# A selective scan's two halves joined into one scan of 1024 columns, with its decays produced two units ahead and half of them kept in SBUF

## The chip, the core and the metric

The kernel runs on one core of a Trainium2 chip. The metric is device time in microseconds (us) of one execution, from the first to the last instruction and what lies around them; lower is better. Three runs of the kernel before gave 3161.89, 3162.53 and 3166.35 us, median 3162.53.

## The reference

The input x has 8 images of 96 channels and 64 x 64 pixels, read as 8 sequences of L = 4096 tokens. Layer 0 is a Mamba block with a residual:

```
u = group_norm(x) as tokens                      # (8, 4096, 96)
xm, z = split(u @ in_proj_w.T)                   # 192 channels each
xm = silu(causal_conv4(xm) + conv_b)
dt, Bm, Cm = split(xm @ x_proj_w.T)              # 6, 16 and 16 columns
delta = softplus(dt @ dt_proj_w.T + dt_proj_b)
h_t = exp(delta_t * A) * h_{t-1} + delta_t * Bm_t * xm_t     # 192 channels x 16 states
y_t = sum over the 16 states of h_t * Cm_t  +  xm_t * D
x = x + layer_norm((y * silu(z)) @ out_proj_w.T)
```

Layer 1 works on the tokens: linear attention without softmax (6 heads; keys times values are summed over a whole sequence), then a feed-forward of 96 to 384 to 96 with weights and activations rounded to 8 and 16 bit floats; both have a layer norm before and a residual.

The recurrence h is what matters here. For each image it has 192 x 16 = 3072 independent rows, each 4096 steps long.

## The kernel before

**Tiling.** Images are taken in pairs (NP = 4 pairs, p), and a sequence in NCH = 8 chunks of T = 512 tokens (c), so there are 32 chunks in a row. Each chunk does its scans in NU = 24 *units* u. `where(u)` (L653) splits u into j (three groups of 64 channels), g (four groups of four states) and b (which image of the pair). A unit works on 128 partitions, four states times 32 channels, and on two halves h (the two sets of 32 channels of the 64), each 512 columns long: 1024 columns in all.

**A unit's work.** In `unit` (L711) a unit u needs:
- its decays `da` = exp(delta * A): two ACT activations of 512 columns (`decay`, L675 to L683). They read `dl`, which DMA has spread over the partitions, and write one PSUM bank each; the tag `da` has two banks, so the decay of half h of unit u+1 is produced as soon as the scan of half h of unit u has read that bank.
- its products `dbu` = delta * x * B: one POOL multiplication of 1024 columns, both inputs in SBUF (`products_b`, L659). It is issued three units ahead (AHEAD = 3) into four buffers, so that of u+3 waits for the scans of u-1.
- its scans: two DVE `tensor_tensor_scan` of 512 columns (L741), one for each half, which read `da` from PSUM and `dbu` from SBUF and write `hs` in SBUF. The first value of a half is 0.0 in the first chunk of a pair and otherwise the last column of the same unit in the chunk before, read from the tile `state`, into which ACT copies the last columns of both halves (L719, L722).
- its products with C: `pr` = hs * cc on DVE (L763), where `cc` is C spread over the partitions by TensorE into PSUM (L671). For the six units in `POOLED` (4, 5, 12, 13, 20, 21) POOL multiplies instead, one unit later (`pooled`, L770), with C spread by DMA into SBUF.
- its sums over the states: TensorE adds the `pr` of a pair of units into the PSUM bank `y` (`sums`, L688 to L698), four matmuls a pair. The sums of units 4 and 5, and of 12 and 13, are issued at units 8 and 16; units 20 and 21 have no such place, so their `pr` is computed and never added. `gate` (L707) then multiplies y by silu(z).

**Order.** The order of the instructions is written out by hand and each engine runs its own in that order. Between the units' own work stand the steps of other stages, by the table `STEPS`: the projections of the chunk after next (P, with Silu and Softplus, which need another table of ACT), the output projection and norms of the chunk before (E), the feed-forward of a chunk nine earlier (F0, F1), the attention's weights (W) and the next pair's group statistics (G). In a unit these come in two parts: part 0 before the scans, part 1 after them. `now("norms")` and `now("others")` release small POOL jobs that were put off. At unit SILU = 10 the decays of unit 12 are put early into the two spare banks `mp` and `mE`, ahead of ACT's Silu.

**PSUM and SBUF.** All eight PSUM banks are in use: cc and da two each, mp, mE, mF and y one each. After the last chunk the rest of E, W and F runs as a tail, in which many lanes of F work at a time and reuse buffers: `x2` takes those of `pr` and `b` in turn.

Of the kernel before, what the change touches and what calls it, by code (L numbers as in the profile page):

```python
# [23 lines left out]
RANK = 6  # L24
POOLED = (4, 5, 12, 13, 20, 21)
POOLED_G = 2
SILU = 10
ROWS_B = (16, 18, 20, 22)
AHEAD = 3

# [35 lines left out]
def tile_mamba_linear_attention_ffn(  # L66
# [41 lines left out]
    def view(t, shape):  # L108
# [8 lines left out]
            t = t.rearrange("p (a b c) -> p a b c", a=shape[1], b=shape[2])  # L117
        return t

    def psum(tag="mp"):  # L120
        return ps_all.tile([128, T], F32, tag=tag, name=tag, bufs=2 if tag in ("cc", "da") else 1)


    ident = const.tile([128, 128], F32, name="ident")
    make_identity(nc, ident)
    mhalf = const.tile([128, 8], F32, name="mhalf")
    nc.vector.memset(mhalf, -0.5)

    def rsqrt(out_, var, eps):

# [98 lines left out]


    def passing(shape, name):
        t = p2.tile([128, 2, T], F32, tag="pr", name=name, bufs=4)
        return view(t, shape)

    gamma = const.tile([128, C], F32, name="gamma")
# [417 lines left out]
    def where(u):  # L653
        return u // (2 * NG), (u // 2) % NG, u % 2
# [17 lines left out]
            cc, lhsT=sel[64:128, g, b], rhs=s["cs"][64:128, :], start=True, stop=True  # L672
        )

    def decay(s, u, h, bank=None):  # L675
        if ("da", u, h) in s:
            return
        j, g, b = where(u)
        da = psum(bank) if bank else ps_all.tile([128, T], F32, tag="da", name="da", bufs=2)
        s["da", u, h] = da  # L680
        nc.scalar.activation(  # L681
            da, s["dl", j][:, 2 * b + h, :], AF.Exp, scale=aneg[:, 2 * j + h, g : g + 1]
        )  # L683


# [22 lines left out]
        zs = s["zs"][:, j, :]  # L708
        nc.vector.tensor_mul(zs, s["y"], zs)  # L709

    def unit(s, prev, nxt, first, u, steps):  # L711
        def at(v):
            return (s, v) if v < NU else (nxt, v - NU)


        if u - 1 in POOLED:
            pooled(s, u - 1)
        if u:
            nc.scalar.copy(state["new"][:, u - 1, :], s.pop(("hs", u - 1))[:, :, T - 1])  # L719
        else:  # L720
            if prev is not None:
                nc.scalar.copy(state["new"][:, NU - 1, :], prev.pop(("hs", NU - 1))[:, :, T - 1])  # L722
            state["last"] = state.get("new")
            state["new"] = p2.tile([128, NU, 2], F32, tag="state", name="state")
        to, v = at(u + 1)
        if to is not None:
            rows_c(to, v)
        if u - 3 in POOLED and u % 2 == 0:
            sums(s, u - 3)
        if u % 2 == 0 and (u or prev is not None) and (u - 1) not in POOLED:  # L730
            sums(s if u else prev, (u or NU) - 1)
        now("norms")
        steps(u, 0)
        to, v = at(u + AHEAD)
        if to is not None:
            products_b(to, v)
        hs = s["hs", u] = p2.tile([128, 2, T], F32, tag="hs", name="hs", bufs=3)
        dbu = s.pop(("dbu", u))
        to, v = at(u + 1)
        for h in range(2):  # L740
            nc.vector.tensor_tensor_scan(  # L741
                hs[:, h, :], s.pop(("da", u, h)), dbu[:, h, :],
                0.0 if first else state["last"][:, u, h : h + 1], ALU.mult, ALU.add,
            )
            if to is not None:
                decay(to, v, h)
        now("others")

        new = u % (2 * NG) == 1
        if new and u > 1:  # L750
            gate(s, u // (2 * NG) - 1)
        elif new and prev is not None:
            gate(prev, NJ - 1)
        if u == SILU and (nxt is not None):
            for h in range(2):
                decay(s, u + 2, h, ("mp", "mE")[h])
        steps(u, 1)
        if new:
            skip(s, u // (2 * NG))
        if u in POOLED:  # L760
            return
        pr = s["pr", u] = p2.tile([128, 2, T], F32, tag="pr", name="pr", bufs=4)
        nc.vector.tensor_mul(  # L763
            pr, hs, s.pop(("cc", u)).unsqueeze(1).to_broadcast([128, 2, T])
        )
# [172 lines left out]
    def chain_f(p, c, b, banks, lane=None):  # L938

        bank = banks[0]  # L940
        x1d, t1d = kept[p, c]
        after = lane is not None

        def place(tag, out_tag, bufs):

            return dict(tag=out_tag, bufs=bufs) if after else dict(tag=tag, bufs=1)

        blk = slice(b * NK, (b + 1) * NK)
        x2 = p2.tile(
            [128, NK, C], F32, name="x2", **place(f"x2{b}", ("pr", "b")[(lane or 0) % 2], 4)  # L950
        )
# [14 lines left out]
        yield  # L966
        x2f = x2.rearrange("p k c -> p (k c)")
        nc.vector.tensor_add(x2f, ps[:, 0 : NK * C], x2f)  # L968
        norm = norm_stats(x2, NK, f"f{b}")
        yield  # L970
        bank = banks[1]
        o2 = p2.tile([128, NK, C], F32, name="o2", **place("o2", "hs", 3))
        for k in range(NK):
            normalise(o2[:, k, :], x2[:, k, :], norm, k)
        yield
        ps = psum(bank)
        for k in range(NK):
            nc.tensor.transpose(ps[0:C, k * 128 : (k + 1) * 128], o2[:, k, :], ident)  # L978
        yield
        qT = p2.tile([C, T], F8, name="qT", **place("qT", "zs", 2))  # L980
        nc.scalar.activation(qT, ps[0:C, :], AF.Copy, saturate=False)
        yield
        h8 = []
        h16 = []
        casts = []

        def hidden(m):
            ps = psum(bank)
            nc.tensor.matmul(
                ps, lhsT=w1T[:, m * 128 : (m + 1) * 128], rhs=qT, start=True, stop=True  # L990
            )
            return ps

        def rounded(m, ps):
            to = dict(tag=("du", "dl")[lane % 2] if after else "h16")
            h16.append(p2.tile([128, T], F16, name="h16", **to))
            nc.scalar.copy(h16[m], ps)  # L997

        def relu(m):
            if not m:  # L1000
                h8.append(p2.tile([128, 3, T], F8, name="h8", **place("h8", "xm", 2)))
            if after:
                nc.vector.tensor_scalar(  # L1003
                    h16[m], h16[m], b1q[:, m : m + 1], 0.0, ALU.add, ALU.max
                )
# [12 lines left out]
        ps = hidden(1)  # L1018
        yield
        rounded(1, ps)  # L1020
        relu(0)
        ps = hidden(2)
        yield
        rounded(2, ps)
        relu(1)
        yield
        relu(2)
        yield
        for job in casts:
            settle(job)  # L1030
        ps = psum(bank)
        for m in range(3):
            nc.tensor.matmul(  # L1033
                ps[0:C, :], lhsT=w2T[:, m, :], rhs=h8[0][:, m, :], start=(m == 0), stop=(m == 2)
            )
        yield
        y16 = p2.tile([C, T], F16, name="y16", **place("y16", "pq", 2))
        nc.scalar.copy(y16, ps[0:C, :])
        if after:
            nc.vector.tensor_scalar(y16, y16, b2q, None, ALU.add)  # L1040
        else:
            nc.scalar.activation(y16, y16, AF.Identity, bias=b2q)
        ps = psum(bank)
        for k in range(NK):
            nc.tensor.transpose(ps[0:C, k * 128 : (k + 1) * 128], x2[:, k, :], ident)  # L1045
        yield
        res = p2.tile([C, T], F32, tag="rows", name="res")
        nc.vector.tensor_add(res, ps[0:C, :], y16)  # L1048
        nc.sync.dma_start(out[2 * p + b, :, c * T : (c + 1) * T], res)
# [62 lines left out]
    with tc.manual_schedule():  # L1112
        for u in range(AHEAD):
            products_b(slots[0], u)
        for h in range(2):
            decay(slots[0], 0, h)
        rows_c(slots[0], 0)
        for i, (p, c) in enumerate(chunks):
            s = slots[i]
# [14 lines left out]
                    step(name, i)  # L1134

            for u in range(NU):
                unit(s, prev, nxt, c == 0, u, steps)

    for kind in list(waiting):
        now(kind)  # L1140
        del waiting[kind]
    s = slots[N - 1]
    sums(s, NU - 1)
    gate(s, NJ - 1)
    rest = [(p, c, b) for p in range(NP) for c in range(NCH) for b in range(2)]
# [81 lines left out]
```

## Time and profile before

| | us | share of the span |
|---|---|---|
| median of three runs | 3162.53 | |
| profiled execution, first to last instruction (span) | 3160.5 | |
| DVE busy | 2935.2 | 93% |
| POOL busy | 2840.7 | 90% |
| PE busy | 2469.6 | 78% |
| ACT busy | 2263.9 | 72% |
| PE weight loads | 928.7 | 29% |
| DMA, mean of 16 engines | | 57% in the main queue |

The engines are PE (TensorE), DVE (VectorE), ACT (ScalarE) and POOL (GpSimd); SP issues most DMAs. An engine's busy time is the union of its instructions, so that two which overlap by their ends are not counted twice. A group's row gives the line of the kernel, the engine, the operation, the tile written and those read, the shape, the count, then the busy time and the mean of one, and at last how long the engine sat idle just before instructions of this group, and what ended that idle time. The first scans start 69.5 us after the first instruction, and the last one ends at 3008.1 us; what follows is the tail. The granted TensorE clock is 0.81 of full speed on average.

### The profile page before, as it was taken

How to read it: one execution, taken by the hardware profiler on the slowest of the kernel's cores; microseconds unless marked ns; L12 is line 12 of the kernel's file. 1: busy time of each engine (PE TensorE's matmuls, PEld its weight loads, DVE VectorE, ACT ScalarE, POOL GpSimd, SP SyncE). 2: the span in 40 equal slices, each digit the busy share in tenths (PEclk: the TensorE clock that was granted, in tenths of full speed). 3: DMA queues.
4: the chain of work that ended last, by engine and by line, in shares of the span. 5: the costliest groups of instructions: out<-in, count | busy, mean ns of one | idle time of the engine just before them, and what ended most of it. 6: DMA issues, size and time to landing. Idle time of an engine off the chain costs nothing. (4 is left out here: it accounts for less than half of the span.)

```text
span 3160.5 us, 35127 instructions
## 1 busy us (share of the span) xinstructions
PE 2469.6 (78%) x9450; PEld 928.7 (29%) x9450; DVE 2935.2 (93%) x4265; ACT 2263.9 (72%) x4360; POOL 2840.7 (90%) x1921
## 2 busy tenths in 40 slices
PE   6787787878787777777777778777888778887777
PEld 2122222222222223222233323222323222332344
DVE  4999999999999999999999999999999999999945
ACT  3666666667677777777777777777877777777656
POOL 2999999999999999999999999999999999999955
PEclk8677777787778888888888877898888888877668
DMA  6655556665555667555667555567565466755322
GB/s 149 152 122 137 134 156 152 160 150 135 141 143 135 138 162 175 146 129 125 141 164 170 141 146 125 137 157 170 146 148 127 124 144 162 169 132 134 95 70 73
DMA packets 253037, 443.75 MB, mean 140 GB/s; under 512 B 37605, under 2 KB 45990, under 8 KB 252838
## 3 DMA queue, kind: packets, MB, share of 16 engines
q1 hardware_dynamic: 247846, 439.40, 56.9%
q10 hardware_dynamic: 4992, 2.11, 0.3%
q8 instruction: 74, 1.21, 0.2%
q14 instruction: 125, 1.02, 0.1%
HBM read 349.11 MB, written 92.27 MB: 140 GB/s over the span
## 5 line engine op out<-in xcount | busy, mean ns | idle before, releaser
L659 POOL TENSOR_TENSOR dbu<-du,b 128x1024 f32<-128x1024 f32 x768 | 1804.6, 2371 | 112.6 <-DVE hs L741 65.5
L741 DVE TENSOR_TENSOR_SCAN hs<-da,state,dbu 128x512 f32<-128x512 f32 x1290 | 1573.5, 1265 | 25.6 <-ACT da L681 24.6
L681 ACT ACTIVATE da<-dl,aneg 128x512 f32<-128x512 f32 x1474 | 1000.6, 688 | 665.4 <-DVE hs L741 644.2
L763 DVE TENSOR_TENSOR pr<-hs,cc 128x1024 f32<-128x1024 f32 x576 | 698.7, 1213 | 35.1 <-DVE hs L741 0.5
L695 PE MATMUL y<-pr,ssum 128*32 128x512 f32 x2816 | 585.1, 831 | 113.3 <-DVE pr L763 113.3
L770 POOL TENSOR_TENSOR pr<-hs,c 128x1024 f32<-128x1024 f32 x192 | 453.8, 2363 | 36.6 <-DVE hs L741 30.4
L459 PE MATMUL mp<-u,wk 96*64 96x512 f32 x1488 | 398.1, 658 | 66.6 <-ACT xm L477 66.4
L671 PE MATMUL cc<-cs,sel 64*128 64x512 f32 x576 | 330.0, 583 | 144.8 <-DVE pr L763 144.4
L671 PEld LDWEIGHTS cc<-cs,sel 64*128 64x128 f32 x576 | 121.6, 215 | 557.3 <-DVE pr L763 296.8
L741 DVE TENSOR_TENSOR_SCAN hs<-da,dbu 128x512 f32<-128x512 f32 x184 | 213.2, 1205 | 17.4 <-POOL dbu L659 9.9
L516 PE MATMUL mp<-dbl,dtT 12*128 12x512 f32 x186 | 158.9, 947 | 56.8 <-ACT cs L506 38.5
L695 PEld LDWEIGHTS y<-pr,ssum 128*32 128x32 f32 x2816 | 87.9, 132 | 380.6 <-DVE pr L763 201.6
L791 PE MATMUL mE<-woT,zs 128*128 128x192 f32 x744 | 146.6, 350 | 66.7 <-ACT t1e L799 45.1
L459 PEld LDWEIGHTS mp<-u,wk 96*64 96x64 f32 x1488 | 97.0, 145 | 293.6 <-issue 156.6
L132 POOL TENSOR_TENSOR rs<-rs,mhalf 128x8 f32<-128x8 f32 (+1 forms) x128 | 173.3, 1354 | 10.7
L791 PEld LDWEIGHTS mE<-woT,zs 128*128 128x128 f32 x744 | 127.3, 200 | 126.8 <-ACT t1e L799 70.5
L703 PE MATMUL y<-xm,dd 128*128 128x512 f32 x192 | 129.2, 760 | 22.4 <-DVE zs L709 21.9
L467 PE MATMUL mp<-u,wz 96*64 96x512 f32 x372 | 137.0, 825 | 4.3 <-ACT xm L485 4.3
L1011 POOL CAST h<-h 128x512 fp8e5<-128x512 f16 x192 | 117.6, 622 | 24.8 <-DVE h L1003 15.8
L719 ACT COPY state<-hs 128x2 f32<-128x2 f32 x736 | 130.1, 181 | 0.2
L420 ACT ACTIVATE o<-x,nm,rs 128x96 f32<-128x96 f32 x256 | 98.6, 455 | 36.4 <-POOL nm L414 34.4
L531 POOL TENSOR_TENSOR du<-delta,xm 128x512 f32<-128x512 f32 x93 | 117.1, 1273 | 0.0
(306 smaller groups left out, 3234.1 us busy)
## 6 DMA issues: line engine op xcount, KB each, us to landing
du<-lu SPq DMA_DIRECT2D x380, 256.0 KB, 5.5
dl<-ld SPq DMA_DIRECT2D x380, 256.0 KB, 7.9
b<-bd SPq DMA_DIRECT2D x512, 128.0 KB, 5.0
lu<-du SPq DMA_DIRECT2D x96, 256.0 KB, 5.7
ld<-delta SPq DMA_DIRECT2D x93, 256.0 KB, 2.4
c<-bd SPq DMA_DIRECT2D x128, 128.0 KB, 4.4
xg<-in_x_dram SPq DMA_DIRECT2D x32, 384.0 KB, 3.8
xr<-in_x_dram SPq DMA_DIRECT2D x32, 384.0 KB, 8.7
```

The source lines that it names most:

```text
L132: nc.gpsimd.tensor_tensor(out_, out_, mhalf[0 : out_.shape[0], 0 : out_.shape[1]], op=ALU.pow)
L459: nc.tensor.matmul(ps[64 * b : 64 * b + 64, :], lhsT=wk[:, k, 64 * j : 64 * j + 64], rhs=u[:, b, k : k + T], start=(k == 0), stop=(k == 3),)
L467: nc.tensor.matmul(ps[64 * b : 64 * b + 64, :], lhsT=wz[:, 64 * j : 64 * j + 64], rhs=u[:, b, 3 : T + 3], start=True, stop=True,)
L516: nc.tensor.matmul(ps, lhsT=dtT[:, j, :], rhs=dbl[0 : 2 * RANK, :], start=True, stop=True)
L659: nc.gpsimd.tensor_mul(dbu, s["du", j][:, 2 * b : 2 * b + 2, :], s["b", g][:, b, :].unsqueeze(1).to_broadcast([128, 2, T]),)
L671: nc.tensor.matmul(cc, lhsT=sel[64:128, g, b], rhs=s["cs"][64:128, :], start=True, stop=True)
L681: nc.scalar.activation(da, s["dl", j][:, 2 * b + h, :], AF.Exp, scale=aneg[:, 2 * j + h, g : g + 1])
L695: nc.tensor.matmul(s["y"][q : q + 32, :], lhsT=ssum, rhs=pr[:, h, :], start=False, stop=(g == NG - 1),)
L741: nc.vector.tensor_tensor_scan(hs[:, h, :], s.pop(("da", u, h)), dbu[:, h, :], 0.0 if first else state["last"][:, u, h : h + 1], ALU.mult, ...
L763: nc.vector.tensor_mul(pr, hs, s.pop(("cc", u)).unsqueeze(1).to_broadcast([128, 2, T]))
L770: nc.gpsimd.tensor_mul(pr, s["hs", u], s["c", g][:, b, :].unsqueeze(1).to_broadcast([128, 2, T]))
L791: nc.tensor.matmul(ps[:, 2 * k * C : 2 * (k + 1) * C], lhsT=zs[:, j, tok : tok + 128], rhs=woT[:, j].rearrange("p b c -> p (b c)"), start= ...
```

## The change

The two scans of a unit become one of 1024 columns over both halves, h = 0 first. To keep the halves apart, the decay of column 0 of the second half is a constant 0.0, written once. The second half's carried state then can't be the scan's first value; instead its share, exp(delta * A) of that column times the carried state, is added into the same column of `dbu` by a one-column ACT activation (`carry`), a unit ahead. The factors for that come from `first_decays`, four small ACT activations for each j of a chunk. In the first chunk of a pair there is nothing to carry.

The decays lie in two fixed tiles, used by turns: even units in PSUM (two banks, as before), odd units in a new SBUF tile `ds`. Those of unit u+2 are issued right after the scan of unit u. The rule for unit SILU goes. To find room in SBUF, the tag `pr` has three buffers in place of four, here, in the constants' set-up and in the tail. The missing sums of units 20 and 21 are added at unit 0 of the next chunk, and after the last chunk, so y now holds these two units' products.

```diff
-SILU = 10
+    das = [
+        ps_all.tile([128, 2, T], F32, tag="da", name="da"),
+        const.tile([128, 2, T], F32, name="ds"),
+    ]
+    for t in das:
+        nc.vector.memset(t[:, 1, 0:1], 0.0)
-        t = p2.tile([128, 2, T], F32, tag="pr", name=name, bufs=4)
+        t = p2.tile([128, 2, T], F32, tag="pr", name=name, bufs=3)
+    def decay(s, u):
         j, g, b = where(u)
+        for h in range(2):
+            nc.scalar.activation(
+                das[u % 2][:, h, h:T], s["dl", j][:, 2 * b + h, h:T], AF.Exp,
+                scale=aneg[:, 2 * j + h, g : g + 1],
+            )
+    def first_decays(s, j):
+        a0 = s["a0", j] = p2.tile([128, NG, 2], F32, tag="a0", name="a0")
+        dl = s["dl", j].rearrange("p (b h) t -> p b h t", h=2)
+        for g in range(NG):
+            nc.scalar.activation(
+                a0[:, g, :], dl[:, :, 1, 0], AF.Exp, scale=aneg[:, 2 * j + 1, g : g + 1]
+            )
+    def carry(s, u, last):
+        j, g, b = where(u)
+        if not u % (2 * NG):
+            first_decays(s, j)
+        to = s["dbu", u][:, 1, 0:1]
         nc.scalar.activation(
+            to, s["a0", j][:, g, b : b + 1], AF.Identity, bias=to, scale=last[:, u, 1:2]
         )
...
+        if u == 0 and prev is not None:
+            sums(prev, NU - 3)
...
-        to, v = at(u + 1)
-        for h in range(2):
-            nc.vector.tensor_tensor_scan(
-                hs[:, h, :], s.pop(("da", u, h)), dbu[:, h, :],
-                0.0 if first else state["last"][:, u, h : h + 1], ALU.mult, ALU.add,
-            )
-            if to is not None:
-                decay(to, v, h)
+        if u + 1 < NU:
+            if not first:
+                carry(s, u + 1, state["last"])
+        elif nxt is not None and not last:
+            carry(nxt, 0, state["new"])
+        nc.vector.tensor_tensor_scan(
+            hs.rearrange("p h t -> p (h t)"),
+            das[u % 2].rearrange("p h t -> p (h t)"),
+            dbu.rearrange("p h t -> p (h t)"),
+            0.0 if first else state["last"][:, u, 0:1], ALU.mult, ALU.add,
+        )
+        to, v = at(u + 2)
+        if to is not None:
+            decay(to, v)
         now("others")
...
-        if u == SILU and (nxt is not None):
-            for h in range(2):
-                decay(s, u + 2, h, ("mp", "mE")[h])
...
         x2 = p2.tile(
-            [128, NK, C], F32, name="x2", **place(f"x2{b}", ("pr", "b")[(lane or 0) % 2], 4)
+            [128, NK, C], F32, name="x2",
+            **place(f"x2{b}", ("pr", "b")[(lane or 0) % 2], 3 + (lane or 0) % 2)
         )
...
+    sums(s, NU - 3)
     sums(s, NU - 1)
```

More of the change, by code (lines that the diff above doesn't have):

```diff
@@ L118, in view @@
         return t
+    das = [
+        ps_all.tile([128, 2, T], F32, tag="da", name="da"),
+        const.tile([128, 2, T], F32, name="ds"),
+    ]
+    turns = [0]
     def psum(tag="mp"):
-        return ps_all.tile([128, T], F32, tag=tag, name=tag, bufs=2 if tag in ("cc", "da") else 1)
+        if tag == "da":
+            turns[0] += 1
+            return das[0][:, turns[0] % 2, :]
+        return ps_all.tile([128, T], F32, tag=tag, name=tag, bufs=2 if tag == "cc" else 1)
     ident = const.tile([128, 128], F32, name="ident")
@@ L673, in rows_c @@
         )
-    def decay(s, u, h, bank=None):
-        if ("da", u, h) in s:
-            return
+    def decay(s, u):
         j, g, b = where(u)
-        da = psum(bank) if bank else ps_all.tile([128, T], F32, tag="da", name="da", bufs=2)
-        s["da", u, h] = da
+        for h in range(2):
[15 more added lines that the diff above has]
+        to = s["dbu", u][:, 1, 0:1]
         nc.scalar.activation(
-            da, s["dl", j][:, 2 * b + h, :], AF.Exp, scale=aneg[:, 2 * j + h, g : g + 1]
+            to, s["a0", j][:, g, b : b + 1], AF.Identity, bias=to, scale=last[:, u, 1:2]
         )
@@ L709, in gate, with unit @@
         nc.vector.tensor_mul(zs, s["y"], zs)
-    def unit(s, prev, nxt, first, u, steps):
+    def unit(s, prev, nxt, first, last, u, steps):
         def at(v):
@@ L761, in unit @@
             return
-        pr = s["pr", u] = p2.tile([128, 2, T], F32, tag="pr", name="pr", bufs=4)
+        pr = s["pr", u] = p2.tile([128, 2, T], F32, tag="pr", name="pr", bufs=3)
         nc.vector.tensor_mul(
@@ L1114, in tile_mamba_linear_attention_ffn @@
             products_b(slots[0], u)
-        for h in range(2):
-            decay(slots[0], 0, h)
+        for u in range(2):
+            decay(slots[0], u)
         rows_c(slots[0], 0)
@@ L1136, in tile_mamba_linear_attention_ffn @@
             for u in range(NU):
-                unit(s, prev, nxt, c == 0, u, steps)
+                unit(s, prev, nxt, c == 0, c == NCH - 1, u, steps)
     for kind in list(waiting):
```

## The prediction

> **What bounds the kernel now.** I read the page's engine shares and its costliest groups first, then the table of busy time by stage, the waits of DVE, and at last the shortest and longest instruction of single lines. The page's groups (line, engine, operation, output from inputs, count; then busy us and mean ns of one; then idle time before them):
>
> ```profile
> L659 POOL TENSOR_TENSOR dbu<-du,b 128x1024 f32<-128x1024 f32 x768 | 1804.6, 2371 | 112.6 <-DVE hs L741 65.5
> L741 DVE TENSOR_TENSOR_SCAN hs<-da,state,dbu 128x512 f32<-128x512 f32 x1290 | 1573.5, 1265 | 25.6 <-ACT da L681 24.6
> L681 ACT ACTIVATE da<-dl,aneg 128x512 f32<-128x512 f32 x1474 | 1000.6, 688 | 665.4 <-DVE hs L741 644.2
> L763 DVE TENSOR_TENSOR pr<-hs,cc 128x1024 f32<-128x1024 f32 x576 | 698.7, 1213 | 35.1 <-DVE hs L741 0.5
> ```
>
> The scans and the products pr fill DVE, which hardly idles; ACT waits 644 us for scans, so it has room. The stages (us, then busy us and count of PE, PEld, DVE, ACT, POOL, then granted clock, DMA share, GB/s): start, body in four stretches, tail.
>
> ```profile
> 0.00:69.50 69.50, 41.85 (x136) 15.92 (x136) 25.70 (x79) 20.63 (x42) 13.21 (x37) 0.93 0.55 136
> 69.50:591.10 521.60, 412.46 (x1411) 131.68 (x1411) 509.66 (x608) 349.13 (x651) 482.50 (x256) 0.75 0.60 144
> 591.10:1512.10 921.00, 720.53 (x2782) 262.33 (x2782) 889.56 (x1226) 671.43 (x1283) 858.51 (x538) 0.82 0.60 146
> 1512.10:2638.00 1125.90, 894.99 (x3540) 335.75 (x3540) 1078.03 (x1546) 862.21 (x1658) 1057.48 (x702) 0.83 0.60 146
> 2638.00:3008.10 370.10, 285.57 (x1067) 109.47 (x1068) 355.30 (x500) 269.49 (x531) 345.14 (x231) 0.76 0.55 133
> 3008.10:3160.50 152.40, 114.16 (x515) 73.58 (x513) 76.93 (x312) 90.99 (x200) 83.85 (x160) 0.75 0.23 70
> ```
>
> In the body (2938.6 us) DVE is busy 2832.6 and POOL 2743.6. DVE sets the pace, and POOL idles only 195.0 us of it. Whatever makes POOL longer by more than that sets a new pace.
>
> **The change, part by part.** The sum is made against the profiled span, 3160.5 us; the median of the runs, 3162.53, lies 2.0 above it.
>
> *One scan in place of two.* Two scans of 512 in a row take 2.45 us by the timeline where they read a carried state and 2.33 where the first value is a constant; one alone takes 1.265 and 1.205, so the second adds 1.19 and 1.13. One scan of 1024 reads no state for its second half: that saves 0.06. It also saves the fixed part of a second instruction. DVE's products take 0.668 at 512 columns (zs, L709) and 1.213 at 1024, so at most 2 x 0.668 - 1.213 = 0.12 is fixed. The saving lies in 0.06 to 0.18 per unit with state (672 of 768) and 0 to 0.12 without (96): 40 to 132 us of DVE. I take the middle, 0.12 and 0.06: 86 us, and 2.33 for the long scan.
>
> *Decays two units ahead.* decay(u+2) still waits for scan u, whose buffer it overwrites, but the scan of u+1 no longer needs it. That aims at the idle time that DVE owes to ACT:
>
> ```profile
> DVE hs L741 <- ACT da L681: 31.7, 43, 1.2
> DVE res L1048 <- ACT da L681: 19.8, 18, 1.7
> ```
>
> So 0 to 51 us more. The rule SILU that goes had prefetched one unit into spare banks (62 decays), which now run in their ordinary turn.
>
> *ACT's additions.* 672 carries of one column and 28 x 3 x 4 = 336 first decays of two columns; the nearest row is the state copy (L719, 128x2), 181 ns: 1008 x 0.181 = 182 us. Half the decays now write SBUF; the nearest such row is the relu of L1007, 720 ns against 688, some 25 us. ACT goes from 2264 to about 2470 us, under POOL and DVE: nothing on the path by itself. The carry of u+1 waits for the product dbu of u+1, and behind it in ACT's queue stand decay(u+2), the state copy and the steps' evictions. When I set each product's end beside the scans in the timeline, the product of u+1 has ended before scan u starts in over nine cases of ten (median 2.9 us before), so today's lead of POOL covers it; if POOL becomes the pace this cover is gone, and ACT runs at POOL's heel.
>
> *The left-out pair.* The sums for units 20 and 21: L695 has 2816 records, 88 per chunk, 8 for a pair. 256 more at 585.1/2816 = 0.21 us are 53 us of PE, spread over chunks whose PE is busy 75 to 80%, and ahead of a gate that waits 4.7 us for PE in the whole run. Cost nothing to 5 us.
>
> *Three pr buffers for four, three x2 buffers in every second lane of the tail.* pr of u+3 needs the sums of u, issued a unit earlier: 0 to 10 us; in the tail a load waits for an older lane: 0 to 5. I take 5 in all, lost in the rest.
>
> *Half the decays in SBUF.* This decides. A scan of an odd unit now has both operands, ds and dbu, in SBUF, while POOL multiplies two SBUF tensors nearly without pause. Every large DVE row of the body today has one input in PSUM (da, cc, y, mE, mF) or only one input, so no row shows such a pair beside a product. From one side: nothing. From the other: the engines exclude each other, as the smallest row of the body shows for a DVE copy within SBUF. (Minimum, median and maximum ns of one, then the POOL instruction beside the slowest copy, and that copy; then POOL beside the last copy, and that copy):
>
> ```profile
> L170 DVE COPY gnm<-gnmv x4: 165/302/2003, 25.4 to 2094.6; 96x2 f32<-96x2 f32 x4
> ```
> ```profile
> 606.12 2.36 POOL L659 TENSOR_TENSOR dbu<-du,b 128x1024 f32<-128x1024 f32 x1 [1.96 <-DMA dl<-ld]
> ```
> ```profile
> 606.50 2.00 DVE L170 COPY gnm<-gnmv 96x2 f32<-96x2 f32 x1
> ```
> ```profile
> 2092.54 4.69 POOL L659 TENSOR_TENSOR dbu<-du,b 128x1024 f32<-128x1024 f32 x2
> ```
> ```profile
> 2094.62 0.30 DVE L170 COPY gnm<-gnmv 96x2 f32<-96x2 f32 x1
> ```
>
> A copy of two columns takes 165 ns at the start, with POOL idle. At 606.50 it meets a product that ends at 606.12 + 2.36 = 608.48, and ends 0.02 us later. At 2094.62 it meets the first of two products in a row; it ends as that one does (half of 4.69) and slips in between. So a product holds something that this copy needs, for its whole length, and DVE gets it at the product's end. The subtraction L176, two SBUF inputs, took 157 ns each time, but it only ever met POOL's power (L132), beside which the tail's relu (L1003) also ran at 353 ns, while beside casts that relu took up to 765. So L176 tells nothing. The row nearest to the new scan is the copy beside a product, so I take exclusion: an odd scan waits for the running product, and POOL stands still for the scan.
>
> The Trainium skill ("SBUF — State Buffer", "Who interferes with whom") says it directly: a DVE instruction with two SBUF inputs and a GpSimd instruction that reads SBUF exclude each other for the whole instruction. By it, the sum is the one below; no run here shows it yet.
>
> **The sum.** POOL stands still 384 x 2.33 = 895 us. Its power rows are 173.3 of 2840.7 us busy, 6%, beside which a scan would cost nothing: -54. Of POOL's 195 us idle, 143 is waiting for DVE's scans and statistics (65.5 + 30.4 + 47.1) and mostly goes when POOL is last; I leave 100 for that and for waits behind the carries. Start 69.5, body 2743.6 + 895 - 54 + 100, tail 152.4, around it 2.0: **3908 us**. DVE would need 2832.6 - 86 + 384 waits of 0 to 2.37 = 2747 to 3657 in the body, under POOL's 3685, so POOL sets the pace and DVE's saving is worth nothing. All idle gone: 3808. All idle kept and nothing free beside the power: 4057.
>
> **The rivals.**
> *No exclusion for two inputs* (the other side: faster). For it: scan and product read at a leisurely pace, over 2 ns a column each, and the copy's case may be its own. Against: the copy's rows. Then 3162.5 - 86 - 51 = 3026 at best; POOL's floor is 69.5 + 2743.6 + 152.4 + 2 = 2968, and with 100 of idle 3068, so DVE and POOL both stand near the limit: 3085, between 3026 and 3130. It decides if an odd scan costs POOL under (195 - 100)/384 = 0.25 us; above that POOL's body outgrows today's.
> *Shared reads without a lock.* A product makes 2048 reads a lane in 2.36 us, 1.15 ns each; if each of the scan's 1024 reads pushes one back, a scan costs POOL 1.18 us, 453 in all: 69.5 + 2743.6 + 453 + 100 + 152.4 + 2 = 3521, between 3300 and 3800.
> *The carry as the new wait.* Without exclusion, scans whose product comes late (about one in 15) wait through ACT: 50 units by up to 1.5 us, 75 us, and the gain shrinks to 3160: no change.
>
> **How the numbers follow.** Exclusion 0.74 (3800 to 4060 its own range, 0.66 within it, the rest above or just under); shared reads 0.10; no exclusion 0.13; carry 0.03, of which 0.02 within 0.2%, about what a measurement of this kernel can tell from no change, and 0.01 slower. Range 3300 to 4060: it holds the first and the second case but for their ends and leaves out the faster one. Faster 0.13, same 0.02, slower 0.85.
>
> **What would show it.** Right: scans from ds far longer than scans from da (toward 3.5 to 4.7 us, or an idle time before them), products of POOL with a mean over 3 us or gaps that end with a scan, POOL over 95% of the body, DVE's share down. Wrong: scans from ds and da alike near 2.33 and products still at 2.37. If the time is near 3500, products are stretched by about 1.2 us only beside scans from ds. I am wrong altogether if ACT is the last to end before scans.

## The result, and the profile after

The kernel after takes 3776.24 us (median of 4 runs, 3772.44 to 3776.61), beside 3162.21 us for the kernel before on the same chip: 1.193 times as long, interval 1.192 to 1.195. Slower, as forecast, inside the range but 132 us short of the 3908 foretold. The profiled execution has a span of 3770.6 us. In the kernel after, the lines have moved: the products `dbu` stand at L669, the scan at L773, POOL's `pr` at L802, the carry at L708.

First the groups of the page, to be held against those of before (busy us, mean ns of one, then idle time before them):

```profile
L669 POOL TENSOR_TENSOR dbu<-du,b 128x1024 f32<-128x1024 f32 x768 | 2174.2, 2852 | 47.3 <-DMA ld<-delta 36.0
L773 DVE TENSOR_TENSOR_SCAN hs<-ds,state,dbu 128x1024 f32<-128x1024 f32 x336 | 1099.6, 3273 | 97.3 <-ACT dbu L708 77.8
L773 DVE TENSOR_TENSOR_SCAN hs<-da,state,dbu 128x1024 f32<-128x1024 f32 x336 | 786.6, 2341 | 109.0 <-ACT dbu L708 77.7
...
L802 POOL TENSOR_TENSOR pr<-hs,c 128x1024 f32<-128x1024 f32 x192 | 607.3, 3163 | 2.5 <-issue 1.2
...
L708 ACT ACTIVATE dbu<-a,dbu,state 128x1 f32<-128x1 f32 x672 | 256.8, 382 | 168.5 <-POOL dbu L669 167.8
```

The same scan instruction takes 2.34 us where its decays lie in PSUM and 3.27 where they lie in SBUF. POOL's products, which have not changed, went from a mean of 2.37 to 2.85 us. The idle time of the products that scans had caused (65.5 us before) is down to 10.5. The stages (us, then busy us of PE, PEld, DVE, ACT, POOL, granted clock, DMA share, GB/s), start, body, tail:

```profile
0.00:70.10 70.10, 41.33 (x136) 15.93 (x136) 25.88 (x81) 21.66 (x44) 13.20 (x37) 0.93 0.52 134
70.10:3622.50 3552.40, 2613.21 (x9053) 919.71 (x9053) 3150.17 (x3108) 2405.85 (x5122) 3496.16 (x1723) 0.72 0.48 119
3622.50:3770.60 148.10, 109.72 (x519) 68.79 (x517) 78.38 (x311) 92.53 (x203) 84.06 (x161) 0.77 0.24 73
```

The whole loss lies in the body, 3552.4 us against 2938.6. POOL is busy in 3496.2 of it, so it idles 56 us: POOL has taken DVE's place as the engine that ends last. The instructions of single lines (minimum, median and maximum ns of one, then the times of the first and last) show that the loss is in the instructions and not between them:

```profile
L773 DVE TENSOR_TENSOR_SCAN hs<-ds,state,dbu x336: 2317/3118/4575, 172.9 to 3620.2; 128x1024 f32<-128x1024 f32 x168
L773 DVE TENSOR_TENSOR_SCAN hs<-da,state,dbu x336: 2317/2343/2352, 169.3 to 3616.6; 128x1024 f32<-128x1024 f32 x168
L669 POOL TENSOR_TENSOR dbu<-du,b x768: 2334/2362/4464, 67.7 to 3607.2; 128x1024 f32<-128x1024 f32 x192
L422 POOL TENSOR_SCALAR nm<-mv x128: 239/258/2596, 202.8 to 3749.0; 128x8 f32<-128x8 f32 x64, 128x4 f32<-128x4 f32 x64
L142 POOL TENSOR_TENSOR rs<-rs,mhalf x128: 1036/1398/1675, 203.5 to 3749.6; 128x8 f32<-128x8 f32 x64, 128x4 f32<-128x4 f32 x64
```

A scan from `da`, with one input in SBUF, takes 2.35 us at most, one from `ds` up to 4.58. A product's shortest and median time are those of an undisturbed one, its longest 2 us more. Even a multiplication of four columns by -1 (L422) can take 2.6 us. Only the power (L142) is untouched in this kernel. What happens is seen in a few us of the timeline (start and length in us), first POOL, then DVE:

```profile
1802.82 2.35 POOL L669 TENSOR_TENSOR dbu<-du,b 128x1024 f32<-128x1024 f32 x1
1805.13 4.35 POOL L802 TENSOR_TENSOR pr<-hs,c 128x1024 f32<-128x1024 f32 x1
1802.90 4.42 DVE L773 TENSOR_TENSOR_SCAN hs<-ds,state,dbu 128x1024 f32<-128x1024 f32 x1 [0.77 <-POOL pr L802]
1807.42 1.22 DVE L795 TENSOR_TENSOR pr<-hs,cc 128x1024 f32<-128x1024 f32 x1
```

The scan starts at 1802.90, while a product runs that ends at 1802.82 + 2.35 = 1805.17. It ends at 1807.32, 2.15 us after that product: an almost whole scan follows the product's end. POOL's next product starts at 1805.13 and ends at 1809.48, 2.16 us after the scan's end: it has waited inside its own instruction in turn. Over the whole run, 293 of the 384 scans that read `ds` ended 2.15 us after a running product's end (90% of these between 2.146 and 2.151), and 268 products that started during such a scan ended 2.14 to 2.18 us after it. These 268 took 4.24 to 4.46 us; the other 692 of the 960 products took 2.33 to 2.39, with none between.

### The profile page after: what moved, and what is told of

Read it like the earlier page. It is cut to its first block, busy times and chain, and to the rows that moved or that the text cites. A ratio compares the mean times of both kernels' runs of the same rounds, so it can differ in the third digit from the quotient of the medians.

```text
span 3770.6 us, 35419 instructions
## 1 busy us (share of the span) xinstructions
PE 2764.3 (73%) x9706; PEld 1004.4 (27%) x9706; DVE 3254.4 (86%) x3499; ACT 2520.0 (67%) x5368; POOL 3593.4 (95%) x1921
## 3 DMA queue, kind: packets, MB, share of 16 engines
q1 hardware_dynamic: 247846, 439.40, 47.1%
## 5 line engine op out<-in xcount | busy, mean ns | idle before, releaser
L669 POOL TENSOR_TENSOR dbu<-du,b 128x1024 f32<-128x1024 f32 x768 | 2174.2, 2852 | 47.3 <-DMA ld<-delta 36.0
L773 DVE TENSOR_TENSOR_SCAN hs<-ds,state,dbu 128x1024 f32<-128x1024 f32 x336 | 1099.6, 3273 | 97.3 <-ACT dbu L708 77.8
L773 DVE TENSOR_TENSOR_SCAN hs<-da,state,dbu 128x1024 f32<-128x1024 f32 x336 | 786.6, 2341 | 109.0 <-ACT dbu L708 77.7
L688 ACT ACTIVATE ds<-dl,aneg 128x512 f32<-128x512 f32 (+1 forms) x768 | 510.9, 712 | 406.2 <-DVE hs L773 396.1
L722 PE MATMUL y<-pr,ssum 128*32 128x512 f32 x3072 | 673.8, 894 | 136.1 <-DVE pr L795 131.6
L688 ACT ACTIVATE da<-dl,aneg 128x512 f32<-128x512 f32 (+1 forms) x768 | 527.6, 687 | 257.0 <-DVE hs L773 207.6
L802 POOL TENSOR_TENSOR pr<-hs,c 128x1024 f32<-128x1024 f32 x192 | 607.3, 3163 | 2.5 <-issue 1.2
L469 PE MATMUL mp<-u,wk 96*64 96x512 f32 x1488 | 519.9, 824 | 58.8 <-ACT xm L487 50.0
L708 ACT ACTIVATE dbu<-a,dbu,state 128x1 f32<-128x1 f32 x672 | 256.8, 382 | 168.5 <-POOL dbu L669 167.8
L142 POOL TENSOR_TENSOR rs<-rs,mhalf 128x8 f32<-128x8 f32 (+1 forms) x128 | 173.2, 1353 | 10.7
L773 DVE TENSOR_TENSOR_SCAN hs<-ds,dbu 128x1024 f32<-128x1024 f32 x48 | 158.7, 3306 | 7.3 <-POOL pr L802 4.7
```

The source lines that it names most:

```text
L142: nc.gpsimd.tensor_tensor(out_, out_, mhalf[0 : out_.shape[0], 0 : out_.shape[1]], op=ALU.pow)
L469: nc.tensor.matmul(ps[64 * b : 64 * b + 64, :], lhsT=wk[:, k, 64 * j : 64 * j + 64], rhs=u[:, b, k : k + T], start=(k == 0), stop=(k == 3),)
L669: nc.gpsimd.tensor_mul(dbu, s["du", j][:, 2 * b : 2 * b + 2, :], s["b", g][:, b, :].unsqueeze(1).to_broadcast([128, 2, T]),)
L688: nc.scalar.activation(das[u % 2][:, h, h:T], s["dl", j][:, 2 * b + h, h:T], AF.Exp, scale=aneg[:, 2 * j + h, g : g + 1],)
L708: nc.scalar.activation(to, s["a0", j][:, g, b : b + 1], AF.Identity, bias=to, scale=last[:, u, 1:2])
L722: nc.tensor.matmul(s["y"][q : q + 32, :], lhsT=ssum, rhs=pr[:, h, :], start=False, stop=(g == NG - 1),)
```

## The experiments

Each was measured beside the kernel before (medians 3163.4 to 3164.2 us). The edits are against the kernel before or the kernel after, as said. Some kernels leave part of the computation out; their expectations say which.

**1. The decays' place alone.** Kernel before, two scans of 512 and all, with three `pr` buffers, and the odd units' decays in SBUF:

```diff
-        da = psum(bank) if bank else ps_all.tile([128, T], F32, tag="da", name="da", bufs=2)
+        if u % 2:
+            da = p2.tile([128, T], F32, tag="ds", name="ds")
+        else:
+            da = psum(bank) if bank else ps_all.tile([128, T], F32, tag="da", name="da", bufs=2)
```

> The kernel before with one part of the change alone: the decays of odd units go to SBUF (two buffers of 512 columns, three pr buffers), while the two scans of 512, the decays one unit ahead and the state read by both scans stay. Theory (a scan with both inputs in SBUF and a POOL product exclude each other): far slower than before, 3900 to 4500 us. POOL can slip a product between the two half scans of an odd unit, so DVE waits twice in it, and DVE itself may set the pace; scans from ds are spread up to about 1.2 + 2.2 = 3.4 us, products up to about 2.36 + 1.0. Rival (the joined scan, the carry or the decays' later place cost the time): 3162 us within 20, products at 2.37.

Measured: 3901.8 us, ratio 1.232 (1.230 to 1.235). This one edit costs more than the whole change. Two groups of its page:

```profile
L744 DVE TENSOR_TENSOR_SCAN hs<-ds,state,dbu 128x512 f32<-128x512 f32 x672 | 1469.8, 2226 | 21.0 <-ACT ds L684 14.6
L744 DVE TENSOR_TENSOR_SCAN hs<-da,state,dbu 128x512 f32<-128x512 f32 x618 | 755.6, 1263 | 0.0
```

A scan from SBUF takes 0.96 us more than one from PSUM, and there are 768 of them: some 740 us. DVE's busy time grew by 759 us (2935.2 to 3694.5), and the kernel lost 738. Here DVE is the engine that ends last (busy 95%, POOL 87%), while POOL ends last in the kernel after. There a unit has one scan that can meet a product and not two, which may be why. The rest of the change wins back 126 us (3901.8 - 3776.2); which part of it does was not tried.

**2. Half the dose.** As run 1, with fewer units:

```diff
-        if u % 2:
+        if u % 4 == 1:
```

> As the run before it, but only the decays of every fourth unit (u % 4 == 1) go to SBUF: half the dose. Exclusion: about half of the extra time of the full dose, less what POOL's 195 us of idle time in the body absorbs, 3450 to 3850 us, and products stretched only beside scans from ds. Rival (a fixed cost of having the tile, such as three pr buffers): the same time as with the full dose. Rival (other parts of the change): 3162 within 20.

Measured: 3570.83 us, ratio 1.128 (1.125 to 1.130). Half as many units in SBUF cost +407 us, 55% of +738. The cost goes nearly with the number of scans that read two SBUF tensors.

**3. The change without the carry.** Kernel after, without `carry` and `first_decays`:

```diff
-        if u + 1 < NU:
-            if not first:
-                carry(s, u + 1, state["last"])
-        elif nxt is not None and not last:
-            carry(nxt, 0, state["new"])
```

> The changed kernel without the carry: the second half's carried state is left out of the product (so h of the second half starts each chunk at zero, which is not the reference's) and 672 + 336 ACT instructions go. Exclusion: POOL sets the pace, so DVE's 155 us of waiting for the carry turns into waiting for POOL: 3730 to 3776 us, POOL's products as in the changed kernel (mean 2.85). Rival (the carry as a chain POOL, ACT, DVE is a main cost): about 3776 - 155 = 3620 us.

Measured: 3778.8 us, ratio 1.194 (1.192 to 1.196); the change itself has 1.193. That is 3 us above the range of the first expectation and far from the rival's. In the kernel after, DVE's scans wait 155.5 us for the carry, its largest wait. Without it DVE's idle time stays what it was (516 us with the carry, 511 without) and goes to other rows (us in total, times, longest):

```profile
DVE x L873 <- POOL t1e L845: 74.6, 32, 2.5
DVE hs L768 <- POOL pr L797: 62.9, 74, 1.0
DVE hs L768 <- POOL dbu L669: 45.5, 20, 11.6
DVE hs L768 <- ACT da L688: 42.0, 24, 1.8
DVE hs L768 <- ACT ds L688: 22.1, 22, 1.1
```

With the carry these five rows had 56.7, 59.4, 20.5, 3.6 and 2.2 us. So the wait went in part to POOL itself and in part to the decays, and not straight from the carry to the product behind it. The carry's row named a messenger: POOL, busy 95% of the span in both runs, sets the time with it and without it.

**4. The pair's sums and the three buffers alone.** Kernel before, with three `pr` buffers and:

```diff
+        if u == 0 and prev is not None:
+            sums(prev, NU - 3)
...
+    sums(s, NU - 3)
```

> The kernel before with two small parts of the change alone: the left-out pair summed (four more matmuls a chunk), and three pr buffers in place of four. Forecast: 3160 to 3168 us; PE gains about 53 us busy, no engine waits longer for it. Rival (PE's late sums hold up the gate or a pr buffer): up to 3215 us.

Measured: 3166.04 us (11 runs), ratio 1.0000 (0.9991 to 1.0009). 256 more matmuls, 28 us more of PE, no change in the time.

**5. The joined scan without SBUF decays.** Kernel after, with both parities in the one PSUM tile, so that the decays of u+1 can only be made once scan u has ended:

```diff
-        const.tile([128, 2, T], F32, name="ds"),
...
-                das[u % 2][:, h, h:T], s["dl", j][:, 2 * b + h, h:T], AF.Exp,
+                das[0][:, h, h:T], s["dl", j][:, 2 * b + h, h:T], AF.Exp,
...
-        to, v = at(u + 2)
+        to, v = at(u + 1)
```

> The changed kernel with all decays in the one PSUM tile: both halves of unit u+1 are made after the scan of u, so the joined scan, the carry and the summed pair stay, and the decays two ahead and the SBUF tile go. Exclusion: no scan has two SBUF inputs, so POOL's products return to a mean of 2.37 and scans to 2.33; the time is set by DVE waiting for two activations (1.38 us and the way there) after each scan, which the product with C covers in 18 units of 24 but for some 0.4 us and not at all in 6: 3350 to 3650 us. Rival (the joined scan or the carry stretches POOL): products still at 2.8 or more.

Measured: 3578.92 us, ratio 1.131 (1.129 to 1.133). The groups of POOL's products and of DVE's scans:

```profile
L668 POOL TENSOR_TENSOR dbu<-du,b 128x1024 f32<-128x1024 f32 x768 | 1805.3, 2361 | 296.5 <-DVE hs L772 243.9 <-DMA ld<-delta 35.6 <-DMA c<-bd 6.4
L772 DVE TENSOR_TENSOR_SCAN hs<-da,state,dbu 128x1024 f32<-128x1024 f32 x672 | 1577.8, 2348 | 408.7 <-ACT da L687 252.9 <-ACT state L745 69.6 <-POOL dbu L668 52.5
```

The products are back at 2.36 us with the joined scan and the carry in place, so these don't stretch POOL. What is lost here is another thing: scans wait for their decays. A joined scan holds both banks until its end, and the change needs the SBUF tile for that reason.

**6. A joined scan with three PSUM banks.** Kernel after, with no SBUF decays: a tile of three banks, even units in banks 0 and 1, odd units in 1 and 2; the third bank comes from `cc`, which keeps one buffer and is filled after the unit's product with C. `pr` has four buffers again. A large number put into one column of `dl` makes the second half's first decay 0. Pooled units keep two scans.

```diff
+    da = ps_all.tile([128, 3, T], F32, tag="da", name="da")
...
-        cc = s["cc", u] = ps_all.tile([128, T], F32, tag="cc", name="cc", bufs=2)
+        cc = s["cc", u] = ps_all.tile([128, T], F32, tag="cc", name="cc", bufs=1)
...
+        h = u % 2 if early else 1 - u % 2
+        nc.scalar.activation(
+            da[:, u % 2 + h, :], s["dl", j][:, 2 * b + h, :], AF.Exp,
+            scale=aneg[:, 2 * j + h, g : g + 1],
+        )
```

> A version without SBUF decays: three PSUM banks (cc gives one of its two up), even units read banks 0 and 1, odd units 1 and 2, so that one half's decay is made two units ahead and only the shared middle bank's after the scan; joined scans in 18 units, two scans in the six pooled ones; the zero in column 0 of the second half comes from a large number written into dl there; carry and summed pair as in the change. Exclusion: products at 2.37, DVE the pace again; joined scans save 432 x 0.12 + 144 x 0.05 = 59 us, the waits for decays go in part: 3080 to 3165 us. Rival (a joined scan needs all its decays early, the late half comes behind other ACT work): 3165 to 3350 us, with DVE waiting for da.

Measured: 3688.47 us, ratio 1.165 (1.163 to 1.166): slower than both theories allowed. POOL's products stay at 2.36 us; DVE is busy 79% and waits:

```profile
DVE hs L771 <- ACT da L688: 236.0, 298, 12.6
DVE pr L793 <- PE cc L678: 137.7, 128, 2.7
DVE hs L771 <- ACT state L744: 112.9, 75, 3.7
```

One decay of the next unit is still made late, and with one `cc` bank the product with C waits for TensorE. The rival had named the late decay, at 186 us at most (3350 - 3164); neither expectation had a term for the one `cc` bank.

**7. Writing decays to SBUF, not reading them.** Kernel before, three `pr` buffers; in odd units ACT also writes the first half's decays into an SBUF tile that nothing reads (384 writes, half as many as in the change).

```diff
+        if u % 2 and not h:
+            ds = p2.tile([128, T], F32, tag="ds", name="ds")
+            nc.scalar.activation(
+                ds, s["dl", j][:, 2 * b + h, :], AF.Exp, scale=aneg[:, 2 * j + h, g : g + 1]
+            )
```

> The kernel before (three pr buffers) with one more ACT activation for each odd unit: a second copy of the first half's decays, into SBUF, that nobody reads; DVE reads PSUM as before. Exclusion by DVE's two SBUF reads: products stay at 2.37, the time at 3160 to 3210 us (384 x 0.69 = 265 us more of ACT, most of it in ACT's idle time). Rival (ACT's writing of decays to SBUF, or SBUF traffic as such, slows POOL): products stretched, about half of the extra time of the change, 3400 or more.

Measured: 3176.93 us, ratio 1.004 (1.003 to 1.006), with 206 us more of ACT.

```profile
L659 POOL TENSOR_TENSOR dbu<-du,b 128x1024 f32<-128x1024 f32 x768 | 1804.0, 2369 | 118.3 <-DVE hs L746 74.7 <-DMA dl<-ld 36.8 <-POOL dbu L659 3.3
```

POOL's row is that of before, 1804.6 us. It is DVE's reading that stops POOL, not ACT's writing.

**8. POOL writes and doesn't read.** Kernel after, with the products replaced by a fill of the same tile:

```diff
-        nc.gpsimd.tensor_mul(
-            dbu, s["du", j][:, 2 * b : 2 * b + 2, :],
-            s["b", g][:, b, :].unsqueeze(1).to_broadcast([128, 2, T]),
-        )
+        nc.gpsimd.memset(dbu, 0.001)
```

> The changed kernel with POOL's products du * B left out: POOL fills dbu with a constant instead (an instruction that writes SBUF and reads none). If only POOL's reads exclude the scan: scans from ds at 2.33 beside these fills, stretched only beside the pooled products and other POOL reads, and DVE sets the pace: 2950 to 3120 us. If any POOL instruction excludes it: scans from ds wait for fills too (up to 1 us more), fills are stretched by up to 2 us.

Measured: 3312.62 us, ratio 1.047 (1.045 to 1.049), above what was expected. The instructions of single lines:

```profile
L770 DVE TENSOR_TENSOR_SCAN hs<-da,state,dbu x336: 2317/2344/2352, 154.4 to 3153.0; 128x1024 f32<-128x1024 f32 x168
L770 DVE TENSOR_TENSOR_SCAN hs<-ds,state,dbu x336: 2323/2346/4374, 158.0 to 3156.6; 128x1024 f32<-128x1024 f32 x168
L669 POOL MEMSET dbu<- x768: 941/951/974, 16.4 to 3141.8; 128x1024 f32 x192
```

The median scan from `ds` is now as short as one from PSUM, and the slowest of the 768 fills takes 0.97 us: an instruction of POOL that only writes doesn't meet the scan. The longest scan is still 4.4 us, beside what is left of POOL's reading (the pooled `pr`, of mean 2.80 us in this run, and the small operations). Taking that out gives an estimate of the change without any exclusion: the `ds` scans have a mean of 2.774 where they read a state, 0.43 over the others, and 2.595 where they don't, 0.32 over; 336 x 0.43 + 48 x 0.32 = 160 us, and 3312 - 160 is about 3152, some 0.4% under the kernel before. With real products in place of the short fills POOL would be far fuller (61% busy here), so the time would rather lie above this.

**9 to 12. The carry where POOL doesn't end last.** Two scans of 512 per unit are kept, all decays stay in PSUM, and the carried state of one or of both halves is folded into `dbu`, so that the scan starts from a constant. This asks whether the folding pays if the exclusion is not there. In 9 (both halves) and 10 (second half), POOL makes the factors with small products, a batch for each j:

```diff
+    def prepare(s, j):
+        t = s["a0", j] = p2.tile([128, NG, 2, 2], F32, tag="a0", name="a0")
...
+        nc.gpsimd.tensor_mul(
+            t, dl.unsqueeze(1).to_broadcast([128, NG, 2, 2]),
...
+        nc.scalar.activation(t, t, AF.Exp)
+    def carry(s, u):
...
+            nc.scalar.activation(
+                to, to, AF.Identity, bias=c0[:, u % (2 * NG), h : h + 1]
+            )
...
-                0.0 if first else state["last"][:, u, h : h + 1], ALU.mult, ALU.add,
+                0.0 if first or h in (0, 1) else state["last"][:, u, h : h + 1], ALU.mult, ALU.add,
```

> The kernel before, with the summed pair and with the carried states of both halves folded into dbu, while the two scans of 512 and their PSUM decays stay. The scans then start from the constant 0.0, 1.205 us each and not 1.265: 1344 x 0.06 = 80 us of DVE. Costs: 1344 one-column ACT activations of 0.28 to 0.38 us (376 to 510 us of ACT, which idles 665 us before decays), 84 x 2 small POOL products (about 40 us of POOL's 195 idle). If ACT's queue holds: 3085 to 3150 us. Rival (ACT, then 84 to 88% busy and waiting for products ahead of decays, becomes the wait): 3165 to 3300.

> As the run before it, but only the second half's state is folded in: 672 x 0.06 = 40 us of DVE saved for 190 to 255 us of ACT: 3125 to 3162 us; rival as there: 3165 to 3220.

Measured: 3516.32 us for both halves, ratio 1.111 (1.109 to 1.112), and 3474.22 for one, 1.098 (1.096 to 1.100). Both expectations missed. DVE's waits and ACT's, of kernel 9:

```profile
DVE hs L783 <- ACT da L681: 357.1, 145, 6.5
ACT a L695 <- POOL a L690: 322.4, 84, 6.8
```

ACT waits 84 times, 28 chunks x 3 groups, some 3.8 us each, for a small product of POOL that stands behind large ones in POOL's queue. The decays stand behind it in ACT's queue, and the scans wait for those. In 11 and 12, ACT makes the first columns' decays itself (the products with the state stay on POOL):

```diff
-        nc.gpsimd.tensor_mul(
-            t, dl.unsqueeze(1).to_broadcast([128, NG, 2, 2]),
...
-        nc.scalar.activation(t, t, AF.Exp)
+                nc.scalar.activation(
+                    t[:, g, :, h], dl[:, :, h, 0], AF.Exp,
+                    scale=aneg[:, 2 * j + h, g : g + 1],
+                )
```

> As e10 (two scans, PSUM decays, the second half's state folded into dbu), but the first columns' decays are made by ACT itself (4 activations of two columns for each j), so ACT no longer waits for POOL's small product in the middle of its queue. In e10 that wait was 311 us of ACT (84 times up to 7 us) and DVE then waited 330 us for da. If that wait was the whole loss: 3474 - 330 = 3145, and with 40 us of DVE saved 3120 to 3165 us. Rival (the carry itself, in front of the decays in ACT's queue, is the wait): 3200 or more, with DVE waiting for da.

> As e9 (both halves' states folded in), with the first columns' decays made by ACT (8 activations for each j). DVE saves 80 us in its scans; ACT gains 1344 x 0.285 + 672 x 0.28 = 571 us and stands at about 2830 of 3160. If only e9's wait for POOL was the loss: 3100 to 3165 us; if ACT is now too full: 3170 to 3260.

Measured: 3319.89 us for one half, ratio 1.049 (1.048 to 1.051), and 3395.53 for both, 1.073 (1.072 to 1.075). The first lies in its rival's range, the second above both of its ranges. ACT's waits in 11, then DVE's:

```profile
ACT a L692 <- DMA dl<-ld: 121.2, 28, 7.0
ACT dbu L710 <- POOL c L700: 119.9, 58, 3.9
DVE hs L783 <- ACT da L681: 182.2, 111, 7.0
DVE zs L738 <- PE y L724: 36.3, 23, 2.5
```

Set beside the kernel before, from one unit's first scan to the next unit's: in the 28 chunks with a carried state most units are 0.06 us shorter, but unit 1 went from 4.08 to 5.31 us, unit 13 from 2.95 to 3.70 and unit 21 from 2.50 to 6.24. These three make 35 + 21 + 105 = 160 us, the others cancel, and the spans differ by 159. Unit 21 is where ACT waits for the DMA that brings `dl`, with the decays of unit 22 behind it in ACT's queue. In unit 13 ACT has four new first decays to make, with the scans' decays behind them; in unit 1 DVE waits for the bank y (36.3 us, before 4.7). ACT's waits for POOL's share `c` cost little: most of them (87.5 of 119.9 us) fall in unit 7, which went from 3.73 to 3.67 us and where ACT had waited for scans before. So the gain of a constant first value is real, and these three places, two of them in ACT's order, take more than it gives. Issuing the new work elsewhere was not tried, and whether the folding can pay stays open.

No kernel here beat the one before.

## Why the prediction was right in kind, and 132 us too high

- **What bounds the kernel.** Right. The forecast said that whatever takes over 195 us of POOL sets a new pace. POOL grew by 752.5 us in the body, and the body by 613.8.
- **The joined scan.** The size was right: the long scan was taken at 2.33 us, and measured medians are 2.343 with a state and 2.282 with a constant. Against 2.45 and 2.33 for two, that saves 0.11 and 0.05, where 0.12 and 0.06 were taken. And, as forecast, it is hidden behind POOL (busy 98% of the body); no run here shows its gain by itself. With the products gone from POOL (8), DVE's busy time less the 160 us of waiting is 3026.1 - 160 = 2866, 69 under before.
- **Decays two units ahead.** Half of what it aims at went: DVE's scans waited 31.7 us for `da` before, and 3.6 us for `da` and 2.2 for `ds` after. The other half did not: `res` waited 19.8 us behind decays before and 39.6 after. Neither matters behind POOL.
- **ACT's additions.** Off the path, as forecast (3), but mis-sized. The state copy's 181 ns has no operand by pointer. The first decays, with a scale by pointer, take 283 ns, and the carry, with scale and bias by pointer, 382. So the additions are 672 x 0.382 + 336 x 0.283 = 352 us and not 182. Overlapping ends hide part of it: ACT's busy time grew by 256 us and not 207. The Trainium skill ("ScalarE: Activation LUTs", "What ACT_TABLE_LOAD costs") states that each pointer operand adds some 93 ns, and these three rows, about 0.1 us apart, agree; I had taken the nearest shape without counting the operands.
- **Pair and buffers.** Right: no measurable change (4). TensorE's part was 28 us and not 53.
- **Half the decays in SBUF.** The mechanism was right, and 1, 2, 5, 7 and 8 show it from several sides: with the place of the decays alone the whole loss comes, with half the dose a bit over half of it; without SBUF decays POOL's products are at 2.36 us; writing alone, by ACT (7) or POOL (8), brings no such waiting. The term was too large. The step "POOL stands still 384 x 2.33 = 895, power -54" gave 841 us; measured are 752.5, or 1.96 a scan. A waiting operation ends 2.15 us after the holder, not 2.33, as if some 0.2 us of its own work were already done by then; and 91 of the 384 scans did not start beside a running product. The power was free, as forecast: its row has 173.2 us, before 173.3, and the 15 scans that started beside a running power took 2.28 to 2.35 us. But that is in part luck of the order: no power started during a scan from `ds` here. In run 8 three did, and took 3.49 to 3.57 us, each ending 1.46 us after its scan; in run 1 the longest took 4.39 (minimum, median and maximum ns, as above):

```profile
L132 POOL TENSOR_TENSOR rs<-rs,mhalf x128: 1036/1351/4393, 212.8 to 3878.6; 128x8 f32<-128x8 f32 x64, 128x4 f32<-128x4 f32 x64
```

The 752.7 us of the page fall on `dbu` (+370), `pr` (+154) and the small operations, which the forecast, a sum over scans, did not tell apart: `nm` L422 +62, `t1e` +57, L141 +54, L424 +24, `du` +22.
- **POOL's idle time.** 100 of 195 was left in the sum, 56 stayed: the waits for scans and statistics went almost wholly (L659's 65.5 us became 10.5, `nm`'s 47.1 became 3.9). With the tail 4 us shorter and the start 1 us longer, the foretold span of 3906 becomes 3906 - 89 - 44 - 4 + 1 = 3770, and 3770.6 was measured. The median lies 5.6 us above that span, where 2.0 were added.
- **The rivals.** No exclusion: refuted by the timeline and by 1. It was also priced too well: 8 gives an estimate of some 3152 or more for it, not 3085, with DVE still waiting for carries (62 us there) and for ACT's other steps. Shared reads without a lock: refuted, since products are not stretched by 1.2 us but are either undisturbed or 2 us longer, and scans wait for their end. The carry as the new wait: refuted for this change by 3. (Its 50 late products were too many: in the trace before, 31 of 767 products ended after the scan of the unit before had started.) In 9 to 12, where POOL doesn't set the pace, the carry's helpers do cost 5 to 11%, far more than the 75 us at which that rival was priced, mostly through ACT's order and not through late products.
- **What would show it.** POOL over 95% of the body: 98%. Products over 3 us in the mean: 2.85 for `dbu`, 3.16 for `pr`. Scans from `ds` toward 3.5 to 4.7 us: mean 3.27, median 3.12, longest 4.58. The kind is right, the size less: 268 of the 960 products were stretched, by 2 us, and a quarter of POOL's loss fell on the small operations.

The Trainium skill ("SBUF — State Buffer", "Who interferes with whom") makes the exclusion a matter of a DVE instruction with two SBUF inputs and a GpSimd instruction that reads SBUF, and excepts one that only writes. Runs 7 and 8 and the timeline agree with it for products and fills, the exception too, and add a length: the one that waits ends 2.15 us after the one that holds, of its own 2.35. For the power they differ: it reads SBUF, and scans that started beside a running one were not stretched.

## What to carry to other kernels

Before an operand of a large VectorE instruction is moved from PSUM to SBUF, look at what its other operand is and what GpSimd reads at that time: if both operands end in SBUF and GpSimd is nearly full, each such instruction can cost much of its own length. Here a scan of 2.34 us cost GpSimd 1.96 us and VectorE 0.94 on average. A small row of the profile whose maximum is ten times its minimum (here a copy of two columns) can show such a lock before the change is made. And a wait's row names the last messenger: take that one away and see whether the wait moves on, before it is blamed.

## What was not expected of the hardware

- The exclusion reaches the smallest operations: a multiplication of four or eight columns by a constant on POOL takes 258 ns in the median and up to 2596 beside a scan, where before the longest was 397. With `t1e` of 384 columns, these small operations grew by 62 + 57 + 54 + 24 = 197 us, a quarter of POOL's 752.7.
- The two engines change places at each instruction's end: in the timeline shown, a scan that met a product got in before POOL's next product, which had started 0.04 us before the first one's end and then waited for the scan.
- The price of moving decays to SBUF differs with which engine ends last: two scans of 512 lost 738 us through DVE, one of 1024 lost 614 through POOL, with 0.96 us a short scan and 1.96 of POOL a long one.
- TensorE's granted clock was lower in most of the slower kernels: 0.81 before, 0.72 in the body after, 0.71 in run 1, 0.77 in run 11. It doesn't go by the time alone: run 8, as long as run 11, kept 0.80. PE's busy time grew from 2469.6 to 2764.3 us, though 256 more matmuls alone gave 28 us (4). PE doesn't end last in any of these; what lowers the clock was not tried.
